# A fused gated block on one core: half of the attention's row transposes by DMA in int16 planes, the sums of |w3| in the last network

## The chip, the cores and the metric

The kernel runs on one core of a Trainium2 chip. The metric is the device time in microseconds of one execution; lower is better. Three executions of the kernel before gave 730.83, 730.84 and 731.93 us, median 730.84.

## The reference

`x` is 8 batches of 256 rows of 512, and the context has the same shape. Four steps each add to `x`, each weighted by the tanh of a gate:

```
x = x + tanh(g_xattn[0]) * long_convolution(ctx, ctx, layernorm(x))      # 32 heads of 8
x = x + tanh(g_ffn[0])   * ternary_network(layernorm(x), w1, w2, w3)     # 512 -> 1408 -> 512
x = x + tanh(g_xattn[1]) * attention(layernorm(x), ctx, mask)
x = x + tanh(g_ffn[1])   * sign_network(layernorm(x), w1, w2, w3)        # 512 -> 2048 -> 512

attention(h, m, mask): softmax(where(mask, h @ m.T / sqrt(512), -1e30)) @ m, zero where no key is valid
sign_network(h, w1, w2, w3):
    h = silu(lin(h, w1)) * lin(h, w2);  return lin(h, w3)
    lin(x, w) = quant(x) @ (sign(w) * mean(|w|)).T          # quant: 8 bits, one scale per 64 values
```

In the last network the mean of |w| is one number for a whole weight matrix. It scales the product from outside: the kernel multiplies by the signs and applies `mean(|w3|)` only where the result is added to `x`.

## The kernel before, in words

There are NT = 16 tiles of 128 rows, kept on the chip in `xs`. Five engines work from instruction streams whose order is that of the program text (`tc.manual_schedule()`): TensorE (PE), VectorE (DVE), ScalarE (ACT), GpSimd (POOL), and the queue of SyncE (SP), which issues nearly all DMAs. A wait in a stream holds all that follows in that stream. Tiles come from pools with a few buffers for each tag; a new tile with a tag waits until the readers of the tile that had its buffer are done.

**Convolution** (the first 182 us). A loop over 32 heads; jobs for the later stages are hung on heads with `job(h, slot, f)`: the statistics of the first rows for the first network (`first_stats`, `first_sqrt`, `first_inverse`, `first_by_act`), its weights, and the sums of |w1| and |w2| of the last network. Before it, `warm(n)` issues matmuls that nothing reads.

**First network** (to about 300 us). A loop over row tiles, each in three `up_block`s and a `down0`. `front_norm(t + 2)` normalises a tile that is used two tiles later, `ln_finish` turns the moments of four row tiles into `rstd` and `nmr` (a Newton iteration on POOL). From its fourth tile on, `w1_signs` also loads the last network's weights through `w1st` (three buffers of 256 KB) and takes their signs on ACT.

**Attention** (about 300 to 372 us). Row tile t goes through these steps, spread over iterations of the loop:
- `normalised3(t)` (ACT) makes the normalised rows; `x_transposed` turns them with four PE transposes into PSUM, and DVE copies them out, scaled by 1/sqrt(512), into `xT`.
- `scores` (PE, L938), `masked` (DVE, L946: adds the mask and takes the maximum), `exponentials` (ACT, L953).
- In the next iteration `e_transposed` turns the exponentials (PE, L959, and a copy by ACT, L961), and `readout` (PE, L967) multiplies them by the values. `residual` (DVE, L222) adds the result one iteration later.
- `load_keys`, `load_values` and `load_mask` fetch each batch of two row tiles. `signs`, `SIGNS[t]` at a time, are the remaining `w1_signs`. For the third matrix (i == 2) each also sums |w| (ACT, L842) into `w1sum3`. After all of them `total_w1(2)`, `spread` (a PE matmul that adds over partitions) and `mean_w1(2)` make the mean, and `gw1` is its product with the gate.

On PE an iteration has the order scores, transposes of e, transposes of x, readout. The first two of four blocks of tile 0 of the last network (`up_products` 0 and 1) are already done at the end of this loop.

**Last network** (372 to 728 us). A loop over the 16 row tiles. `up_products(xT, f)` for f = 0 to 3 makes the two products of 512 columns each (`pa`, `pb`) with the left side split in two parts, `hi` and `lo`; there are four PSUM banks for them (`ps_mm`), each freed by Silu (ACT, L1168) or by `up_gate` (DVE, L1172). After f = 1 and f = 3 `half_quantised` quantises half of the hidden row: DVE's scales and int16 values; on SP the scales' row to DRAM (`d`, L1293), the transpose of the values by DMA (`qT`, L1314) and two loads that spread the scales (`sT`, L1301). In tile t + 1 `hidden_high` makes `v = qT * sT` in the pool `p4` (tag `v`, two buffers), ACT's cast makes `hi`, DVE makes `lo`; `down` then multiplies the hidden rows of tile t - 1 by w3. So PE in tile t does up 0 to 3 of tile t and then `down` of tile t - 1. `finish` applies `gw1`, for the first time in tile 2.

```
            if t == 0:
                nxtT = split(pk, turned, "x1")
            g = up_products(xT, 3)
...
            halves.append(half_quantised(hh, 1))
            if 0 < t < NT - 1:
                po = new_out()
                down(po, hT, first if t == NT - 2 else range(NB))
```

The functions that the diff touches:

Of the kernel before, what the change touches and what calls it, by code (L numbers as in the profile page):

```python
# [9 lines left out]
F32 = mybir.dt.float32  # L10
# [3 lines left out]
I16 = mybir.dt.int16  # L14
# [7 lines left out]
P = 128  # L22
# [16 lines left out]
GRP = 4  # L39
# [3 lines left out]
def flamingo_gated_kernel(  # L43
# [115 lines left out]

    def ln_finish(got, g, tag):  # L160

        mv = got[g]
        v = small.tile([P, GRP], F32, tag="nwv", name="nwv")
        nc.vector.tensor_scalar(v, mv[:, :, 1], LN_EPS, None, ALU.add)
        i = small.tile([P, GRP], I32, tag="nwi", name="nwi")
        nc.vector.tensor_scalar(i, v.bitcast(I32), 1, None, ALU.arith_shift_right)
        y = small.tile([P, GRP], F32, tag="rstd" + tag, name="rstd")
        nc.vector.tensor_scalar(  # L170
            y.bitcast(I32), i, -1.0, float(0x5F3759DF), ALU.mult, ALU.add
        )
        w = small.tile([P, GRP], F32, tag="nwt", name="nwt")
        for _ in range(3):
            nc.gpsimd.tensor_tensor(w, y, y, ALU.mult)  # L175
            nc.gpsimd.tensor_tensor(w, w, v, ALU.mult)
            nc.gpsimd.tensor_scalar(w, w, -0.5, 1.5, ALU.mult, ALU.add)
            nc.gpsimd.tensor_tensor(y, y, w, ALU.mult)
        nmr = small.tile([P, GRP], F32, tag="nmr" + tag, name="nmr")
        nc.gpsimd.tensor_tensor(nmr, mv[:, :, 0], y, ALU.mult)  # L180
        nc.gpsimd.tensor_scalar(nmr, nmr, -1.0, None, ALU.mult)
        got[g] = (mv, y, nmr)

    def ln_some(got, order, k, tag):
        ln_moments_of(got, order, k, tag)
        if k % GRP == GRP - 1:
            ln_finish(got, k // GRP, tag)

# [429 lines left out]
    for k, h in enumerate(steps1):  # L618
        job(max(h - 2, steps1[k - 2] if k > 1 else 0), "late", load_w1a, k)
        job(h, "act2", abs_w1, k)  # L620
        if k % N1 == N1 - 1:
# [17 lines left out]

    for k, h in enumerate((24, 25, 28, 29)):  # L640
        job(h, "late", first_by_act, GRP + k)

# [28 lines left out]
    )  # L671
    warm(10)

# [135 lines left out]
    assert not jobs  # L809
    load_table(AF.Silu)  # L810

# [5 lines left out]

    ps_mm.tile([P, 512], F32, tag="mm", name="passed")

# [10 lines left out]
    def w1_signs(k):  # L830


        n = FF1 * L // P // 512
        i, c = k // n, k % n
        st = p_st.tile([P, 512], F32, tag="w1st", name="w1st")
        nc.sync.dma_start(out=st, in_=w1_part(i, c, 512))
# [29 lines left out]
    def down0(hqT):  # L866
# [17 lines left out]
        0: (st0, 1, "0"), 4: (st0, 2, "0"), 8: (st0, 3, "0"),  # L884
        13: (st3, 0, "3"), NT: (st3, 1, "3"),
    }
# [37 lines left out]
    def x_transposed(xn, by_act=False):  # L924
        tr = ps_tr.tile([P, NL, P], F32, tag="tr", name="tr3")
        for c in range(NL):
            nc.tensor.transpose(tr[:, c, :], xn[:, c * P : (c + 1) * P], ident)  # L927
# [55 lines left out]
    for t in range(NT + 1):  # L983
        new = t + 2 < NT
        if t < NT:
            hh = p2.tile([P, FF0], F32, tag="hh", name="hh")
        if new:
            front_norm(t + 2)
# [42 lines left out]
        if t > 2:  # L1031
            hqT, f3 = hq_.pop(t - 2)
            d_[t - 2] = (down0(hqT), f3)
        if t in FINISH:
            ln_finish(*FINISH[t])
# [17 lines left out]
        sums = []  # L1053
        if t == 0:
            clip_by_act(2, 3)
        if t == 3:
# [95 lines left out]
    def up_products(xT, f):  # L1152

        f0 = f * 512
        pa = ps_mm.tile([P, 512], F32, tag="mm", name="pa4")
        pb = ps_mm.tile([P, 512], F32, tag="mm", name="pb4")
        for i, pp in ((0, pa), (1, pb)):
            for c in range(NL):
                for k in range(2):
                    nc.tensor.matmul(  # L1160
# [16 lines left out]

    SIGNS = [2, 2, 2, 2, 1, 2, 1, 1, 2, 1, 2, 1, 1, 1, 1]
    e_, r_ = {}, {}
    for t in range(NT + 2):  # L1180
        if t >= 2:
            residual(t - 2, *r_.pop(t - 2))
        if t < NT and t not in ps_:
            ps_[t] = scores(xT_.pop(t), keys[t // 2])
        if 1 <= t <= NT:
            e, den = e_.pop(t - 1)
# [9 lines left out]
        if 1 <= t <= NT:  # L1196
# [12 lines left out]
        for make in signs:  # L1209
            make()  # L1210
        signs = []
        if t == NT:
            spread(("1", 2))
            up_gate(hh[:, 512:1024], *up_products(xT, 1))
# [12 lines left out]
        if t + 2 * GRP < NT:  # L1227
            ln_some(st3, natural, t + 2 * GRP, "3")
        elif t < 3 * GRP:
            ln_some(st4, natural, t - 2 * GRP, "4")  # L1230
# [7 lines left out]
        else:  # L1238
# [3 lines left out]
            if b + 1 < B:  # L1242
                negs[b + 1] = key_mask(bytes_.pop(b + 1))
        if t == NT - 1:
            total_w1(2)
        if t == NT:
            mean_w1(2)
            nc.vector.tensor_scalar(gw1, wmean1[:, 2:3], gate_f[1], None, ALU.mult)
        if t < len(SIGNS):
            signs = [w1_signs(made + k) for k in range(SIGNS[t])]  # L1250
            made += SIGNS[t]
# [19 lines left out]
    with ExitStack() as ph:  # L1271
# [89 lines left out]


        first, second = range(NB // 2), range(NB // 2, NB)
        prev, sums = None, []
        for t in range(NT):
# [6 lines left out]
            if t > 0:  # L1372
# [97 lines left out]
```

## Time and profile before

| | |
|---|---|
| median of three executions | 730.84 us |
| the profiled execution, its own time | 729.76 us |
| its span, first to last instruction | 728.0 us |
| PE busy | 716.1 us |
| DVE / ACT / POOL busy | 602.4 / 373.8 / 258.4 us |
| one attention iteration (readout to readout) | 4.39 us |
| tile of the last network on PE | 21.76 us |
| DMA, mean of the span | 136 GB/s |

A profiled execution has one clock from the start of the span; all moments in this text are on it. The busy shares say how full an engine is; the chain of waits goes back from the last instruction to whatever released each step; the timeline lists one engine's instructions with start, duration, line, output and inputs, and, in brackets, how long the engine idled before and for whom. The stretches give the busy time of each engine in a window, then the granted PE clock, the share of the DMA engines and the GB/s.

### The profile page before, as it was taken

The numbers are of one execution on the slowest core, as the hardware profiler recorded it, in microseconds if no ns is written. First come the engines' busy times: TensorE is split into PE (matmuls) and PEld (weight loads), VectorE is DVE, ScalarE is ACT, GpSimd is POOL, SyncE is SP. The second block draws the span as 40 slices with busy tenths as digits, with TensorE's granted clock in tenths as the row PEclk, the third lists the DMA queues.
The fourth block names the chain that finished last, engine by engine and source line by source line (L and its number), as shares of the span: only waits on it lengthen the run. The fifth ranks groups of instructions, "written<-read, shape, count | busy, mean of one in ns | idle before, by whom it ended". The sixth has DMA issues, their size and how long they took to land.

```text
span 728.0 us, 10153 instructions
## 1 busy us (share of the span) xinstructions
PE 716.1 (98%) x3212; PEld 533.8 (73%) x3212; DVE 602.4 (83%) x1224; ACT 373.8 (51%) x672; POOL 258.4 (36%) x363
## 2 busy tenths in 40 slices
PE   8999999999999999999999999999999999999997
PEld 7777777776454444566678788888888888888885
DVE  5799888998889887787867988988888988777965
ACT  5677887877778787777742322322212332212322
POOL 4888997989884525443300020000200002000000
PEclk9999999999999999999999999999999999999999
DMA  5774676831136576687605544555544544555443
GB/s 196 253 235 153 194 260 208 280 84 29 36 85 145 141 150 185 149 283 218 203 1 97 115 107 105 110 99 109 119 111 84 110 107 101 113 115 96 97 90 86
DMA packets 149970, 99.36 MB, mean 136 GB/s; under 512 B 83806, under 2 KB 127838, under 8 KB 149918
## 3 DMA queue, kind: packets, MB, share of 16 engines
q1 hardware_dynamic: 149608, 98.38, 53.5%
q0 software_dynamic: 256, 0.26, 0.4%
q8 instruction: 25, 0.41, 0.2%
q14 instruction: 27, 0.22, 0.1%
q10 hardware_dynamic: 54, 0.08, 0.1%
HBM read 75.58 MB, written 5.03 MB: 111 GB/s over the span
## 4 chain that ended last, share of the span: by engine, by line
PE 88%; DVE 4%; DMA 2%; ACT 2%; issue 1%; POOL 1%; SPq 0%; DVEq 0%; ACTq 0%
PE y L343 20%; PE po L1345 16%; PE pb L1160 15%; PE pa L1160 15%; PE po L869 5%; PE po L967 4%; PE pa L852 4%; PE pb L852 4%; PE ps L938 3%; PE tr_back L418 1%; DMA hqT<-qh 1%; DMA w1st<-in_L_w3t 1%; DVE am L512 1%; PE tr L927 1%; PE tr L410 1%
## 5 line engine op out<-in xcount | busy, mean ns | idle before, releaser
L343 PE MATMUL y<-kv,toep 128*128 128x288 f32 x640 | 160.7, 407 | 1.6 <-DVE rstd L128 0.8
L343 PEld LDWEIGHTS y<-kv,toep 128*128 128x128 f32 x640 | 119.3, 190 | 34.3 <-ACT y L353 2.1
L1168 ACT ACTIVATE sl<-pa,wmean 128x512 f32<-128x512 f32 x64 | 44.0, 688 | 187.5 <-PE pa L1160 187.5
L1160 PE MATMUL pa<-w,hi 128*128 128x512 f32 x256 | 100.6, 393 | 0.0
L1160 PE MATMUL pb<-w,hi 128*128 128x512 f32 x256 | 99.7, 390 | 0.4 <-DVE hh L1172 0.4
L1345 PE MATMUL po<-w,lo 128*128 128x512 f32 x256 | 99.9, 390 | 0.0
L1345 PE MATMUL po<-w,hi 128*128 128x512 f32 x256 | 99.6, 389 | 0.0
L1160 PE MATMUL pa<-w,lo 128*128 128x512 f32 x256 | 99.6, 389 | 0.0
L1160 PE MATMUL pb<-w,lo 128*128 128x512 f32 x256 | 99.6, 389 | 0.0
L175 POOL TENSOR_TENSOR nwt<-rstd 128x4 f32<-128x4 f32 x33 | 6.6, 199 | 241.5 <-DVE rstd L170 239.7
L320 POOL TENSOR_TENSOR kv<-cx 128x1024 f32<-128x1024 f32 x32 | 60.6, 1895 | 22.9 <-ACT cx L307 22.7
L852 PEld LDWEIGHTS <-xqT 128*128 128x128 bf16 x384 | 37.5, 98 | 40.0 <-issue 3.0
L388 POOL TENSOR_TENSOR prod<-prod 128x1024 f32<-128x1024 f32 x28 | 66.3, 2367 | 0.4 <-DVE prod L378 0.4
L1135 ACT CAST hi<-v 128x512 fp32r<-128x512 f32 x64 | 39.1, 621 | 48.3 <-DVE v L1335 48.3
L1172 DVE SCALAR_TENSOR_TENSOR hh<-pb,wmean,sl 128x512 f32<-128x512 f32 x64 | 47.7, 745 | 14.2 <-PE pb L1160 14.2
L1345 PEld LDWEIGHTS po<-w,lo 128*128 128x128 f32 x256 | 48.1, 188 | 10.9 <-DVE lo L1140 1.0
L1160 PEld LDWEIGHTS pb<-w,hi 128*128 128x128 f32 x256 | 48.0, 188 | 10.8 <-DVE hh L1172 0.8
L1160 PEld LDWEIGHTS pa<-w,hi 128*128 128x128 f32 x256 | 48.1, 188 | 10.4 <-issue 0.5
L1160 PEld LDWEIGHTS pa<-w,lo 128*128 128x128 f32 x256 | 48.1, 188 | 10.3 <-DVE lo L1140 0.2
L1160 PEld LDWEIGHTS pb<-w,lo 128*128 128x128 f32 x256 | 48.1, 188 | 10.0
L1345 PEld LDWEIGHTS po<-w,hi 128*128 128x128 f32 x256 | 48.0, 188 | 9.9
L365 DVE TENSOR_TENSOR prod<-y,qx 128x512 f32<-128x512 f32 x64 | 43.7, 683 | 9.3 <-ACT y L353 4.0
(160 smaller groups left out, 1350.8 us busy)
## 6 DMA issues: line engine op xcount, KB each, us to landing
sT<-d SPq DMA_DIRECT2D x64, 256.0 KB
toep<-ssm_skip SPq DMA_DIRECT2D x31, 256.0 KB
ch<-in_ctx_heads SPq DMA_DIRECT2D x32, 128.0 KB
w1a<-in_L_w1t SPq DMA_DIRECT2D x8, 512.0 KB
w1a<-in_L_w2t SPq DMA_DIRECT2D x8, 512.0 KB
w1st<-in_L_w1t SPq DMA_DIRECT2D x16, 256.0 KB
w1st<-in_L_w2t SPq DMA_DIRECT2D x16, 256.0 KB
cT<-in_ctx_t SPq DMA_DIRECT2D x8, 512.0 KB
```

The source lines that it names most:

```text
L320: nc.gpsimd.tensor_tensor(kv[:, :, 0 : ND * HD].rearrange("p a (i d) -> p a i d", d=ND), cx[:, :, 0:HD].unsqueeze(3).to_broadcast([P, NL * ...
L343: nc.tensor.matmul(y[:, k, :, W0 : W0 + NPAIR], toeps[h][:, d * P : (d + 1) * P], kvs[h][:, mi * B : (mi + 1) * B, :].rearrange("p b n -> ...
L365: nc.vector.tensor_tensor(prod[:, 0, r, :, :], yv[:, :, W0 : W0 + ND * HD].rearrange("p a (i d) -> p a i d", d=ND), view(q, [HX, n], [1, H ...
L388: nc.gpsimd.tensor_tensor(flat[0], flat[0], flat[1], ALU.add)
L852: nc.tensor.matmul(pp[:, :fw], xqT[:, c, :], w0q[i][:, c, f0 : f0 + fw], start=(c == 0), stop=(c == NL - 1),)
L869: nc.tensor.matmul(po, hqT[:, c, :], w0q[2][:, c, :], start=(c == 0), stop=(c == NF0 - 1))
L967: nc.tensor.matmul(po, eT[:, c, :], cN[:, c, :], start=(c == 0), stop=(c == S // P - 1))
L1135: nc.scalar.copy(hi, v)
L1160: nc.tensor.matmul(pp, xT[k][:, c, :], w1q[i][:, c, f0 : f0 + 512], start=(c == 0 and k == 0), stop=(c == NL - 1 and k == 1),)
L1168: nc.scalar.activation(sl, pa, AF.Silu, scale=wmean1[:, 0:1])
L1172: nc.vector.scalar_tensor_tensor(hh, pb, wmean1[:, 1:2], sl, op0=ALU.mult, op1=ALU.mult)
L1345: nc.tensor.matmul(po, hT[b][k][:, c, :], w1q[2][:, b * NL + c, :], start=(b == 0 and c == 0 and k == 0), stop=(b == NB - 1 and c == NL - ...
```

## The change

- In the attention, row tiles 4 to 15 are no longer turned by PE. POOL splits the normalised float32 rows into two planes of 2-byte integers, the low and the high halves of each value (`x_planes`); one DMA transpose on SP turns both (`x_turned`); DVE copies one plane and ACT the other back into float32 words (`x_merged`). The factor 1/sqrt(512), which the copy out of PSUM applied, goes into `rstd` and `nmr` in `ln_finish` for these rows (two more POOL instructions per group of four).
- `e_transposed` comes ahead of `scores` in iterations 1 to 15.
- The Abs sums of w3 leave `w1_signs`. In the last network `sums_of_w3` loads w3 a second time, 16 parts of 256 KB into the tag `v`, and sums each on ACT: parts 0 to 3 after the first half of tile 0, 4 to 7 after its second half, 8 to 15 after the second half of tile 1, followed by `total_w1(2)`, `spread`, `mean_w1(2)` and `gw1`.
- `SIGNS` is redistributed (the same sum), and signs wait one more iteration at the start.
- `up_products` goes over all four `hi` parts and then over the four `lo` parts.
- Smaller: the heads of `first_stats` and the like in the convolution; `warm(10)` becomes `warm(4)`; the Silu table is loaded by an activation that writes a PSUM tile; in tile 0 of the first network `front_norm(2)` and `ln_finish` come later.

```diff
-    def ln_finish(got, g, tag):
+    def ln_finish(got, g, tag, factor=None):
...
+        if factor is not None:
+            for v in (y, nmr):
+                nc.gpsimd.tensor_scalar(v, v, factor, None, ALU.mult)
...
-    for g, h in enumerate((22, 25)):
-        for k in range(2):
-            job(h + k, "dve", first_stats, 2 * g + k)
-        job(h + 1, "late", first_sqrt, g)
-        job(h + 2, "dve", first_inverse, g)
+    for g, (h0, h1, h2) in enumerate(((19, 21, 23), (23, 24, 28))):
+        job(h0, "dve", first_stats, 2 * g)
+        job(h1, "dve", first_stats, 2 * g + 1)
+        job(h1, "late", first_sqrt, g)
+        job(h2, "dve", first_inverse, g)
...
-    for k, h in enumerate((24, 25, 28, 29)):
-        job(h, "late", first_by_act, GRP + k)
+    for k, at in enumerate(((24, "late"), (25, "late"), (29, "act"), (30, "act"))):
+        job(*at, first_by_act, GRP + k)
...
-    warm(10)
+    warm(4)
...
-    load_table(AF.Silu)
...
-    ps_mm.tile([P, 512], F32, tag="mm", name="passed")
+    passed = ps_mm.tile([P, 512], F32, tag="mm", name="passed")
+    nc.scalar.activation(passed[:, :1], ln_eps, AF.Silu)
...
             nc.scalar.activation(dst, st, AF.Sign)
-            if i == 2:
-                nc.scalar.activation(st, st, AF.Abs, accum_out=w1sum3[:, c : c + 1])
...
+    def x_planes(xn):
+        pl = pt3.tile([P, 2, L], I16, tag="pl", name="pl")
+        nc.gpsimd.tensor_copy(pl, xn.bitcast(I16).rearrange("p (n k) -> p k n", k=2))
+        return pl.rearrange("p k n -> p (k n)")
+
+    def x_turned(pl):
+        bT = pt3.tile([P, 2 * NL, P], I16, tag="bT", name="bT")
+        nc.sync.dma_start_transpose(out=bT, in_=pl)
+        return bT.rearrange("p (k c) m -> p k (c m)", k=2)
+
+    def x_merged(b):
+        xT = p3.tile([P, NL, P], F32, tag="xT", name="xT")
+        v = xT.rearrange("p c m -> p (c m)").bitcast(I16).rearrange("p (n k) -> p k n", k=2)
+        nc.vector.tensor_copy(v[:, 1], b[:, 1])
+        nc.scalar.copy(v[:, 0], b[:, 0])
+        return xT
...
-        if new:
+        if new and t > 0:
             front_norm(t + 2)
...
             up_block(*x0[t], hh, 0)
+        if t == 0:
+            front_norm(t + 2)
...
         for i, pp in ((0, pa), (1, pb)):
-            for c in range(NL):
-                for k in range(2):
+            for k in range(2):
+                for c in range(NL):
...
-    SIGNS = [2, 2, 2, 2, 1, 2, 1, 1, 2, 1, 2, 1, 1, 1, 1]
+    SIGNS = [1, 2, 2, 2, 2, 2, 1, 1, 2, 1, 2, 1, 1, 1, 1]
...
     for t in range(NT + 2):
+        if t + 2 in pl_:
+            bT_[t + 2] = x_turned(pl_.pop(t + 2))
+        if t == NT - 2:
+            xT_[t + 1] = x_merged(bT_.pop(t + 1))
+        if 1 <= t <= NT:
+            e, den = e_.pop(t - 1)
+        if 1 <= t < NT:
+            eT = e_transposed(e)
         if t >= 2:
             residual(t - 2, *r_.pop(t - 2))
         if t < NT and t not in ps_:
             ps_[t] = scores(xT_.pop(t), keys[t // 2])
...
-        if t + 2 < NT:
+        if t + 2 < GRP:
             xT_[t + 2] = x_transposed(xn_.pop(t + 2))
         if t < NT:
             e_[t] = exponentials(*s_nmx)
-        if t + 3 < NT:
+        if t + 1 in bT_ and t < NT - 2:
+            xT_[t + 1] = x_merged(bT_.pop(t + 1))
+        if t + 3 < GRP:
             xn_[t + 3] = normalised3(t + 3)
-        for make in signs:
-            make()
-        signs = []
+        elif t + 3 < NT:
+            pl_[t + 3] = x_planes(normalised3(t + 3))
+        if t > 0:
+            for make in signs:
+                make()
+            signs = []
...
-        if t == NT - 1:
-            total_w1(2)
-        if t == NT:
-            mean_w1(2)
-            nc.vector.tensor_scalar(gw1, wmean1[:, 2:3], gate_f[1], None, ALU.mult)
...
+        def sums_of_w3(cs):
+            for c in cs:
+                st = p2.tile([P, NL, P], F32, tag="v", name="w3st").rearrange("p c m -> p (c m)")
+                nc.sync.dma_start(out=st, in_=w1_part(2, c, 512))
+                nc.scalar.activation(st, st, AF.Abs, accum_out=w1sum3[:, c : c + 1])
...
             halves = [half_quantised(hh, 0)]
+            if t == 0:
+                sums_of_w3(range(0, 4))
...
             halves.append(half_quantised(hh, 1))
+            if t == 0:
+                sums_of_w3(range(4, 8))
+            if t == 1:
+                sums_of_w3(range(8, 16))
+                total_w1(2)
+                spread(("1", 2))
+                mean_w1(2)
+                nc.vector.tensor_scalar(gw1, wmean1[:, 2:3], gate_f[1], None, ALU.mult)
             if 0 < t < NT - 1:
                 po = new_out()
                 down(po, hT, first if t == NT - 2 else range(NB))
```

More of the change, by code (lines that the diff above doesn't have):

```diff
@@ L181, in ln_finish, with ln_some @@
         nc.gpsimd.tensor_scalar(nmr, nmr, -1.0, None, ALU.mult)
+        if factor is not None:
+            for v in (y, nmr):
+                nc.gpsimd.tensor_scalar(v, v, factor, None, ALU.mult)
         got[g] = (mv, y, nmr)
-    def ln_some(got, order, k, tag):
+    def ln_some(got, order, k, tag, factor=None):
         ln_moments_of(got, order, k, tag)
         if k % GRP == GRP - 1:
-            ln_finish(got, k // GRP, tag)
+            ln_finish(got, k // GRP, tag, factor)
     def ln_apply(o, t, mv, rstd, j):
@@ L884, in flamingo_gated_kernel @@
         0: (st0, 1, "0"), 4: (st0, 2, "0"), 8: (st0, 3, "0"),
-        13: (st3, 0, "3"), NT: (st3, 1, "3"),
+        13: (st3, 0, "3"), NT: (st3, 1, "3", scale),
     }
@@ L1033, in flamingo_gated_kernel @@
             d_[t - 2] = (down0(hqT), f3)
-        if t in FINISH:
+        if t in FINISH and t > 0:
             ln_finish(*FINISH[t])
@@ L1054, in flamingo_gated_kernel @@
         if t == 0:
+            ln_finish(*FINISH[t])
             clip_by_act(2, 3)
@@ L1174, in up_gate @@
         )
-    SIGNS = [2, 2, 2, 2, 1, 2, 1, 1, 2, 1, 2, 1, 1, 1, 1]
-    e_, r_ = {}, {}
+    SIGNS = [1, 2, 2, 2, 2, 2, 1, 1, 2, 1, 2, 1, 1, 1, 1]
+    e_, r_, pl_, bT_ = {}, {}, {}, {}
+    pt3 = pool(s_att, "p3turn", 2, reuse_waits="tile")
     for t in range(NT + 2):
+        if t + 2 in pl_:
[6 more added lines that the diff above has]
+            eT = e_transposed(e)
         if t >= 2:
@@ L1185, in flamingo_gated_kernel @@
         if 1 <= t <= NT:
-            e, den = e_.pop(t - 1)
             fac = small.tile([P, 1], F32, tag="fac", name="fac")
@@ L1195, in flamingo_gated_kernel @@
             up_gate(hh[:, 0:512], *up_products(xT, 0))
-        if 1 <= t <= NT:
+        if t == NT:
             eT = e_transposed(e)
@@ L1206, in flamingo_gated_kernel @@
             e_[t] = exponentials(*s_nmx)
-        if t + 3 < NT:
+        if t + 1 in bT_ and t < NT - 2:
+            xT_[t + 1] = x_merged(bT_.pop(t + 1))
+        if t + 3 < GRP:
             xn_[t + 3] = normalised3(t + 3)
-        for make in signs:
-            make()
-        signs = []
+        elif t + 3 < NT:
[4 more added lines that the diff above has]
+            signs = []
         if t == NT:
-            spread(("1", 2))
             up_gate(hh[:, 512:1024], *up_products(xT, 1))
@@ L1227, in flamingo_gated_kernel @@
         if t + 2 * GRP < NT:
-            ln_some(st3, natural, t + 2 * GRP, "3")
+            ln_some(st3, natural, t + 2 * GRP, "3", scale)
         elif t < 3 * GRP:
@@ L1243, in flamingo_gated_kernel @@
                 negs[b + 1] = key_mask(bytes_.pop(b + 1))
-        if t == NT - 1:
-            total_w1(2)
-        if t == NT:
-            mean_w1(2)
-            nc.vector.tensor_scalar(gw1, wmean1[:, 2:3], gate_f[1], None, ALU.mult)
         if t < len(SIGNS):
-            signs = [w1_signs(made + k) for k in range(SIGNS[t])]
+            signs += [w1_signs(made + k) for k in range(SIGNS[t])]
             made += SIGNS[t]
```

## The prediction

> **What bounds the kernel now.** I read the page's busy shares first, then the chain of waits, then the timelines of TensorE (PE), ScalarE (ACT), VectorE (DVE) and the SP queue around the attention and the first tiles of the last network.
>
> ```profile
> PE 716.1 (98%) x3212; PEld 533.8 (73%) x3212; DVE 602.4 (83%) x1224; ACT 373.8 (51%) x672; POOL 258.4 (36%) x363
> PE 88%; DVE 4%; DMA 2%; ACT 2%; issue 1%; POOL 1%; SPq 0%; DVEq 0%; ACTq 0%
> ```
>
> PE is busy for 98% of the span and carries 88% of the chain that ends last. So a saving counts only if it takes PE work away or closes one of PE's few gaps, and whatever makes PE wait is paid in full. One attention iteration on PE:
>
> ```profile
> 335.41 1.98 PE L967 MATMUL po<-cN,eT 128*128 128x512 f32 x4
> 337.23 1.89 PE L938 MATMUL ps<-cT,xT 128*128 128x256 f32 x8
> 338.95 0.38 PE L959 MATMUL tre<-ident,s 128*128 128x128 f32 x2
> 339.17 0.60 PE L927 MATMUL tr<-ident,xn 128*128 128x128 f32 x4
> 339.80 1.98 PE L967 MATMUL po<-cN,eT 128*128 128x512 f32 x4
> ```
>
> From readout to readout it is 4.39 us; the four transposes of x take 0.44 of it in the chain. The last network before the change, first SP and then ACT:
>
> ```profile
> 383.90 0.69 SPq L1293 DMA_DIRECT2D d<-sq  x1
> 385.19 1.25 SPq L1314 DMA_TRANSPOSE qT<-qh  x1
> 386.62 1.34 SPq L1301 DMA_DIRECT2D sT<-d  x2
> ...
> 377.80 0.69 ACT L1168 ACTIVATE sl<-pa,wmean 128x512 f32<-128x512 f32 x1 [1.70 <-PE pa L1160]
> 383.19 0.69 ACT L1168 ACTIVATE sl<-pa,wmean 128x512 f32<-128x512 f32 x1 [4.70 <-PE pa L1160]
> 385.45 0.59 ACT L1135 CAST hi<-tr 128x512 fp32r<-128x512 f32 x1 [1.57 <-PE tr L1149]
> 387.30 0.69 ACT L1168 ACTIVATE sl<-pa,wmean 128x512 f32<-128x512 f32 x1 [1.26 <-PE pa L1160]
> ```
>
> SP issues in the order of the program: the row `d`, the transpose `qT`, the two `sT`. ACT idles a lot there, but it too runs in program order, and each Silu (`sl`) and cast (`hi`) is what PE needs next.
>
> **What the Trainium skill says.** "DMA: Bandwidth & Descriptors", in Anatomy of one DMA: "any semaphore wait happens on the issuing sequencer before dispatch". The trace agrees: in the waits of the SP queue, line L836 (the weight loads) stands 11.1 us behind ACT's sums at L842. The same section fits a DMA of the gpsimd path as 2.0 us plus bytes/436 GB/s, an estimate of 2.6 us for 256 KB. This trace, for SP's queue:
>
> ```profile
> 212.87 2.15 SPq L836 DMA_DIRECT2D w1st<-in_L_w1t  x2
> 213.50:214.00 0.50, 0.50 (x4) 0.20 (x3) 0.43 (x3) 0.50 (x2) 0.50 (x1) 1.00 0.04 5
> 214.00:214.50 0.50, 0.50 (x5) 0.21 (x3) 0.35 (x2) 0.50 (x2) 0.50 (x1) 1.00 0.38 135
> 217.00:217.50 0.50, 0.50 (x5) 0.24 (x3) 0.47 (x3) 0.45 (x1) 0.41 (x2) 1.00 0.26 98
> ```
>
> The issue starts at 212.87, the bytes (last column, GB/s) at 214.0, and the two loads of 256 KB, one after the other, are through at 217.4: 1.1 us to the first byte, about 1.7 us each. I take **2.8 us** from issue to landing; bounds 2.3 (bytes at the 390 GB/s of other stretches) and 5.1 (the `w1st` DMA that the chain shows at 318.54, in traffic). "TensorE: Matmul & The Clock Gate", Part 1: after an idle window of about 3.4 us PE runs at half rate until about 3.4 us of work have passed. The trace agrees in kind: the warming matmuls of 128x128 run 0.216 us apart (20 in 4.31 us), the same shape at L927 later 0.109.
>
> **The sums of |w3|, moved.** Before, each of 16 loads of `w3` (`w1st`) feeds both a Sign and an Abs on ACT (0.72 us with its accumulator read) during the attention. After, the Abs are gone from there, and 16 new loads of 256 KB feed 16 Abs in tiles t=0 and 1 of the last network. They share tag `v`, two buffers, so load k waits on SP for sum k-2; they stand on SP behind `d`, `qT`, `sT` of the half just quantised, and on ACT ahead of the next Silu. I walk it on the clock of the trace before.
>
> *Tile 0, sums 0 to 3.* SP is free at 388.0 (386.62 + 1.34). The engines move `sT` until 390.6 (the stretches there), so loads 0 and 1 land at 391.3 and 392.0. Sums 0 and 1 end at 392.05 and 392.8; loads 2 and 3 go out then and land 2.8 later; sum 3 ends at 396.35. Only now ACT reaches the Silu that ran at 383.19, then the cast that ran at 385.45: done at 397.65. PE had four PSUM banks ahead and finishes `up_products` 3 at 389.1; the first product of tile 1 needs that cast. PE starts at 397.7: **8.6 us late**.
>
> *Sums 4 to 7.* DVE, behind the Silu, multiplies gate 3 from 399.3; as before, 4.07 us later the half is quantised (403.4), then `qT` 1.25 and `sT` 1.3 with the 0.35 between them: SP is free at 406.3. The engines move `sT` to 408.7, load 4 lands at 409.4, sum 5 ends at 410.85, loads 6 and 7 land at 412.95 and 413.7, sum 7 ends at 414.4. ACT's first Silu of tile 1 follows, to 415.1. PE has done two `up_products` (3.63 each) by 405.0 and waits for a PSUM bank until 415.1: **10.1 us**.
>
> *Sums 8 to 15, then `total_w1`, `spread`.* PE finishes products 2 and 3 of tile 1 at 422.4. DVE was held too (the `v` of `hidden_high` wait for the same buffers): from 414.5 it does two `v`, gate, two `lo`, two `v`, gate, the first half's quantising (3.2), two `lo`, gate, `xn`, statistics, gate, `lo` to 427.5, by the durations of its timeline before; the second half is quantised at 430.6, SP is through `sT` at 433.5. Load 8 lands at 436.6, and four pairs follow, each at 2.8 + 0.72 (+0.05): sum 15 ends at 448.7. The reduce (0.17), the matmul `tot` (0.28) and hand-offs: 449.3. `spread` stands on PE **ahead of** `down`, which ran at 404.30 before: everything after is **45.0 us** later. From there PE is dense in both kernels, so nothing is won back. Restarting cold: first restart hidden in the second wait, second behind DVE, third counts 3.4/2 = 1.7 us (bounds 0 and 4). The later `gw1` and 4 MB more traffic cost nothing else: the first use of `gw1` is tile 2, behind the wait already counted.
>
> **The attention.** For 12 rows PE loses four transposes: 12 x 0.44 = 5.3 us at most. The copy `eT` after the transpose of the exponentials, which ends just when the transposes of x do, would stand open; moving `e_transposed` ahead of `scores` (1.73) covers it. New iteration on PE: 1.98 + 1.73 + 0.23 = 3.95. Who else must fit in 3.95?
> - DVE: row 4.39 minus its gaps is near 3.7; `xT` (0.69) is replaced by an int16 copy of 512 elements, not in the trace. I take 0.6, bounds 0.3 and 0.7, nearest row the 0.69 of L1107. Fits.
> - ACT: `eT` 0.44, exponentials 0.6, normalising 0.7, the other plane 0.65 (as L1135), Signs 0.64 each, no Abs: 3.7 with two Signs. Its order makes `eT` late with two, period about 4.0 to 4.1.
> - POOL: `x_planes`, 1024 elements, not in the trace: 1.0 (rate of L1018, 1408 in 1.36) to 1.9 (L320, 1024 in 1.90); I take 1.4. With masks and `ln_finish` under 3.5. The two more multiplies of `ln_finish` are 0.4 per four rows, hidden by the 3 to 6 us POOL idles before it.
> - DMA: a transpose of this size is `qT`, issued in 1.25 and through in 2.7 us, about 1.5 us of all engines. Keys and values 1.3, signs' loads 0.67 each: 3.5 with one Sign, 4.1 with two.
> - SP's order: `x_turned` precedes the next keys and w-loads; a loop row, plane, transpose, merge takes 7 to 9 us for two iterations.
>
> So I take 4.05 instead of 4.39: 12 x 0.34 = **4 us gained**, bounds 5.3 gained and 3 lost.
>
> **The small edits together.** Six fewer warming matmuls (PE stood in them until 10.0 while the first normalised row was there about 8.0), `front_norm` behind the first Silu, `ln_finish` behind the first block, the statistics of conv spread: PE's gaps there are 0.8 (167.9), 0.95 (182.7), 0.2, 0.6 (193.1) and up to 2 at the start. **2 us gained**, bounds 0 and 4.5. The new order hi, then lo in `up_products`: nothing, `lo` is already there in all but one tile. `SIGNS` keeps its sum.
>
> **Sum.** 45.0 + 1.7 - 4 - 2 = +40.7 on the profiled execution's own 729.76 (span 728.0 and 1.76 around it) = 770.5. That execution lies 1.1 below the median of 730.84; I forecast **771**.
>
> **Rivals.**
> - *Only the last wait is open* (ACT is through its sums of tile 0 before PE needs it): 771 - 18.7 = 752. For it: ACT idles 4.7 us before 383.19. Against: the loads can't be issued before 388.0. 0.05.
> - *The sums are hidden, the kernel is faster*: only the gains count, 730.84 - 6 = 725. One mechanism decides, the in-order SP queue with its two buffers: if the loads ran ahead so that sum 15 ended before PE leaves `up_products` of tile 1 at 404.3, nothing waits. For it: DMA is about half busy and ACT 30% there. Against: SP's order in the trace, 45 us too late by my walk. 0.06.
> - *The attention does not gain* (transposes land late and hold `scores`, or DMA is the bound): 771 + 7 = 778. For it: DMA shares near 1.0 at 320 to 331. 0.07.
> - My forecast, own range 758 to 786: 0.82.
>
> A measurement of this kernel can tell about 0.2% (1.5 us) from no change. Faster 0.06, same 0.01, slower 0.93. The range: low end, 8 round trips at 2.3 (-4), all gains at their bounds (-3.8), no cold restart (-1.7) and part of the first wait hidden (-9); high end, round trips a microsecond longer (+8), no gain in the attention (+7), a colder PE (+2): 752 to 788.
>
> **What would show it.** PE idle three times in the last network's first two tiles, about 9, 10 and 27 us, released by ACT `hi`, ACT `sl` and the `tot` matmul's DVE total; `v<-in_L_w3t` loads on SP in pairs 3.6 us apart; ACT waiting for that DMA; attention rows 4.0 us apart. It is wrong if PE stays dense between 372 and 412, or if the gap ahead of `down` is under 15 us.

## The result, and the profile after

Four executions of the changed kernel took 788.18 to 789.57 us, median **789.01 us**, against 730.84 for the kernel before: a ratio of 1.0796, 95% interval 1.0781 to 1.0811. The change costs 58 us. The profiled execution has a span of 787.0 us instead of 728.0, and a mean PE clock of 0.971.

The page of the kernel after, the busy shares first, then two rows of the 40 slices (19.7 us each; busy share of PE and PE's granted clock, both in tenths), then the chain by engine:

```profile
PE 718.2 (91%) x3139; PEld 532.3 (68%) x3152; DVE 598.3 (76%) x1224; ACT 380.6 (48%) x684; POOL 272.3 (35%) x381
...
PE   7999999999999998888954159999999999999997
...
PEclk9999999999999999999977769999999999999999
...
PE 71%; DMA 7%; DVE 6%; POOL 6%; issue 4%; ACT 4%; SPq 1%; ACTq 0%; DVEq 0%; POOLq 0%
```

PE did not get more work: its busy time is 2.1 us above the 716.1 of before, in a span 59 us longer. It lost its cover: 71% of the chain instead of 88%. In the row of PE the slices with 5, 4, 1 and 5 are one place, 393 to 472 us, and there the clock is at 7, 7, 7 and 6 tenths. The three waits, from PE's timeline of that place (start, duration, line, what; in brackets how long PE idled before it and for whom):

```profile
407.26 2.07 PE L1183 MATMUL pa<-w,hi 128*128 128x512 f32 x4 [9.72 <-ACT hi L1157]
426.20 2.08 PE L1183 MATMUL pa<-w,hi 128*128 128x512 f32 x4 [9.94 <-ACT sl L1191]
460.46 0.56 PE L218 MATMUL tot<-wtot,ones 128*128 128x1 f32 x2 [24.53 <-DVE wtot L213]
```

Together 44.2 us of idle PE. What PE waited for, from the chain of waits of the same stretch (start, duration, what):

```profile
396.28 4.85 DMA w3st<-in_L_w3t
401.21 0.73 ACT w3st L1399 x2
401.96 2.70 DMA w3st<-in_L_w3t
404.74 0.66 ACT w3st L1399 x2
...
443.14 4.45 DMA w3st<-in_L_w3t
447.68 0.73 ACT w3st L1399 x2
448.42 2.75 DMA w3st<-in_L_w3t
...
456.36 2.96 DMA w3st<-in_L_w3t
459.40 0.73 ACT w3st L1399 x2
460.46 0.56 PE tot L218 x2
461.02 9.33 PE po L1376 x32
```

Load, sum, load, sum: with two buffers each pair of loads starts when a sum of the pair ahead of it has ended. `down` (the last line) took 9.33 us here and 7.25 in the kernel before, although it is the same 32 matmuls:

```profile
404.30 7.25 PE po L1345 x32
```

PE starts it cold here: on its timeline the first matmuls lie 0.43 us apart, and from 465.2 on 0.23. The waits of the stretch (total, times, longest):

```profile
ACT w3st L1399 <- DMA w3st<-in_L_w3t: 49.8, 11, 14.3
...
DVE wtot L213 <- ACT w3st L1399: 19.7, 1, 19.7
```

Where the 59.0 us of span came from, by the moments at which PE starts the first product of each stage, each rounded to a tenth:

| stage | before | after | difference |
|---|---|---|---|
| convolution, to its last product | 181.3 | 185.2 | +3.9 |
| from there to the first product of the first network | 1.4 | 0.2 | -1.2 |
| first network, to the first `scores` | 115.7 | 117.9 | +2.2 |
| attention, to the first `up_products` | 72.8 | 76.6 | +3.8 |
| to the first `down` | 32.9 | 81.0 | +48.1 |
| the rest | 323.9 | 326.1 | +2.2 |

### The profile page after: what moved, and what is told of

Read it like the earlier page. It is cut to its first block, busy times and chain, and to the rows that moved or that the text cites. A ratio compares the mean times of both kernels' runs of the same rounds, so it can differ in the third digit from the quotient of the medians.

```text
span 787.0 us, 10144 instructions
## 1 busy us (share of the span) xinstructions
PE 718.2 (91%) x3139; PEld 532.3 (68%) x3152; DVE 598.3 (76%) x1224; ACT 380.6 (48%) x684; POOL 272.3 (35%) x381
## 4 chain that ended last, share of the span: by engine, by line
PE 71%; DMA 7%; DVE 6%; POOL 6%; issue 4%; ACT 4%; SPq 1%; ACTq 0%; DVEq 0%; POOLq 0%
PE po L1376 15%; PE y L346 14%; PE pa L1183 14%; PE pb L1183 14%; PE po L869 4%; DMA w3st<-in_L_w3t 4%; PE pa L852 4%; PE pb L852 3%; POOL prod L391 1%; DMA hqT<-qh 1%; PE po L986 1%; PE ps L957 1%; POOL kv L323 1%; DMA bT<-pl 1%; DMA xs<-in_x 1%
## 5 line engine op out<-in xcount | busy, mean ns | idle before, releaser
L1183 PE MATMUL pa<-w,hi 128*128 128x512 f32 x256 | 71.5, 402 | 19.7 <-ACT sl L1191 9.9
L1183 PE MATMUL pa<-w,lo 128*128 128x512 f32 x256 | 70.0, 396 | 0.0
L1183 PE MATMUL pb<-w,hi 128*128 128x512 f32 x256 | 69.0, 392 | 0.0
L1183 PE MATMUL pb<-w,lo 128*128 128x512 f32 x256 | 68.5, 390 | 0.0
L1183 PEld LDWEIGHTS pb<-w,lo 128*128 128x128 f32 x256 | 48.1, 188 | 10.0
```

Source lines behind the costliest of these rows:

```text
L1183: nc.tensor.matmul(pp, xT[k][:, c, :], w1q[i][:, c, f0 : f0 + 512], start=(c == 0 and k == 0), stop=(c == NL - 1 and k == 1),)
```

## The experiments

My theory (A) was the prediction's: the sums of w3 as they stand in the last network cost nearly all, by SP's order and two buffers; the open question was the attention, which did not gain as forecast. The rival (B) for each part is in the expectations. All ratios are against the kernel before, run on the same chip.

**1. The sums alone, both ways.** `e1_sums_only` is the kernel before with only the sums moved; `e2_sums_back` is the kernel after with only the sums put back into the attention.

```diff
             nc.scalar.activation(dst, st, AF.Sign)
-            if i == 2:
-                nc.scalar.activation(st, st, AF.Abs, accum_out=w1sum3[:, c : c + 1])
...
+            if t == 0:
+                sums_of_w3(range(0, 4))
...
+            if t == 1:
+                sums_of_w3(range(8, 16))
+                total_w1(2)
+                spread(("1", 2))
+                mean_w1(2)
```

> The kernel before with only the sums of w3 moved to the last network, as in the change. Theory A (three waits in tiles 0 and 1, as walked in the prediction): PE idles about 9.7, 9.9 and 24.5 us there, down starts about 48 us later than before, restart cold adds 2; the whole takes about 780 us (+50). Rival B (the moved sums cost much of it through ACT or DMA traffic all along, or the attention without its sums wins some of it back): under 770 us, or waits of another length.

> The changed kernel with the sums of w3 put back into the attention, as before. Theory A: the three waits vanish, what is left is the loss up to the end of the attention, 4.9 us before it and 4.0 in it, so about 740 us, or a few us more if ACT's sums (0.72 each) make the copies of the exponentials later still. Rival B (the attention and the small edits are a gain that the sums only hide): 725 to 729 us.

Measured: e1 782.06 us, ratio 1.0702 (1.0682 to 1.0721); e2 740.17 us, ratio 1.0142 (1.0111 to 1.0172). So the move of the sums is worth about +51 us in the kernel before and, taken out of the kernel after, 49; all other edits together, with the sums where they were, are worth **+9**, not a gain. In e1, with none of the other edits present, PE's timeline has the same three waits with the same releasers: 9.34 us for ACT `hi`, 8.82 for ACT `sl`, and this one:

```profile
456.18 0.56 PE L215 MATMUL tot<-wtot,ones 128*128 128x1 f32 x2 [24.21 <-DVE wtot L210]
```

**2. The two buffers.** `e8_sums_hidden` is e1 with other loads: parts 0 to 7 go out ahead of the last network's loop into tiles of the hidden blocks that are idle there, parts 8 to 15 into the same tiles later; the sums are spread over tiles 0 and 1. `e9_after_hidden` does the same to the kernel after.

```diff
-                st = p2.tile([P, NL, P], F32, tag="v", name="w3st").rearrange("p c m -> p (c m)")
-                nc.sync.dma_start(out=st, in_=w1_part(2, c, 512))
+                tag = ("hih", "loh")[c % 2] + str(c // 2 % 4)
+                w3st[c] = p1.tile([P, 512], F32, tag=tag, name="w3st")
+                nc.sync.dma_start(out=w3st[c], in_=w1_part(2, c, 512))
...
+        load_w3(range(8))
```

> The kernel before with the sums of w3 in the last network, but with their loads ahead: parts 0 to 7 are loaded before tile 0 into tiles that are idle until tile 1 (hi and lo of the hidden blocks), parts 8 to 15 as soon as these are summed, and the sums stand behind Silus after which ACT is idle. Theory A (the moved sums cost only through in-order waits for late loads): the three waits vanish, 729 to 733 us, the same as before within 0.3%. Rival B (16 sums and 4 MB more traffic there cost by themselves): 740 us or more.

> The changed kernel with the same loads ahead. Theory A: what remains of the change is the attention (3.9 us longer than before), the first network (about 2 longer) and the end of the convolution (about 1 shorter): 735 to 738 us. Rival B (without the waits the change is a gain): under 729 us.

Measured: e8 741.15 us, ratio 1.0145 (1.0130 to 1.0160); e9 746.01 us, ratio 1.0212 (1.0196 to 1.0227). Of the 51 us, 41 are gone with the same 4 MB and the same Abs: most of the price was loads and sums that waited for each other in order. The run changes both the buffers of the loads and the places of the sums on ACT, so it does not part these two. Some 10 us stayed: I had expected at most 733 for e8 and 738 for e9, and e8 lies in the range of its rival (740 or more). The chain of waits of e8 says where:

```profile
383.48 0.08 SPq L1362
...
383.61 4.70 DMA w3st<-in_L_w3t
...
398.42 5.06 DMA d<-sq
...
404.29 4.78 DMA sT<-d
...
409.80 0.69 DVE v L1327
...
411.20 3.76 PE pb L1158 x8
```

The burst of eight loads could not leave "ahead of the loop": it went out only at 382.8 to 383.5, when the last residual of the attention released the memory that those tiles take over. From there it stood in front of everything else in the queue: the row of scales `d`, which is small, needed 5.06 us to land (in the kernel before, the loads that wait for it go out 2.7 and 3.1 us after its issue). The loads `sT` behind it took 4.78, little more than the 4.50 of the same step before. PE waits 6.2 us for that (6.07 in e9, at the same place), and its next eight matmuls, cold, take 3.76 us (1.84 before). The loads are hidden from ACT and come out again as late scales: the same queue, another victim.

**3. The planes.** `e7_planes_undone` is the kernel after with rows 4 to 15 turned by PE again, `scores` still behind `e_transposed`; the two additional multiplies of `ln_finish` go too (not shown).

```diff
-        if t + 2 < GRP:
+        if t + 2 < NT:
             xT_[t + 2] = x_transposed(xn_.pop(t + 2))
...
-        if t + 3 < GRP:
+        if t + 3 < NT:
             xn_[t + 3] = normalised3(t + 3)
-        elif t + 3 < NT:
-            pl_[t + 3] = x_planes(normalised3(t + 3))
```

> The changed kernel with the rows turned by PE again (x_transposed for all), everything else as changed: the transposes of e ahead of scores, no sums of w3 in the attention, the new SIGNS. Theory A (the planes are what costs): the attention takes 72 to 73 us as in the kernel before, the whole about 4 us less than the changed kernel, 785 us. Rival B (the new order, e_transposed ahead of scores, costs): it stays near 76.6 us, 789.

Measured: 779.38 us, ratio 1.0672 (1.0640 to 1.0704), and an attention of 69.7 us, against 76.6 with the planes and 72.8 before. **Taking the four transposes off PE in this way made the attention 6.9 us longer.** (Each of these figures is from one profile. The same attention differs by up to 0.8 us between profiles: 72.8 before and 73.2 in e3, 72.3 in e10 and 73.1 in e11.) In e7 a row on PE, from its timeline:

```profile
348.28 1.88 PE L986 MATMUL po<-cN,eT 128*128 128x512 f32 x4
...
351.95 0.60 PE L927 MATMUL tr<-ident,xn 128*128 128x128 f32 x4
352.38 1.88 PE L986 MATMUL po<-cN,eT 128*128 128x512 f32 x4
```

4.10 us, and no wait. The kernel after, same view, three of its waits:

```profile
342.20 1.98 PE L986 MATMUL po<-cN,eT 128*128 128x512 f32 x4 [1.52 <-ACT eT L980]
...
357.26 2.00 PE L957 MATMUL ps<-cT,xT 128*128 128x256 f32 x8 [0.84 <-ACT xT L951]
...
360.71 1.99 PE L986 MATMUL po<-cN,eT 128*128 128x512 f32 x4 [1.46 <-ACT eT L980]
```

**4. Why the planes are late.** Two candidates: the DMA queue (the Signs' loads `w1st` and the transposes share it) and the order of POOL. `e5_no_w3_loads` leaves out 15 of the 16 `w1st` loads of w3; `e6_short_newton` takes two of three Newton steps from `ln_finish` for the rows from 4 on; `e6b_short_no_loads` does both.

```diff
-        st = p_st.tile([P, 512], F32, tag="w1st", name="w1st")
-        nc.sync.dma_start(out=st, in_=w1_part(i, c, 512))
+        if i == 2 and c > 0:
+            st = kept[0]
...
-        for _ in range(3):
+        for _ in range(1 if tag == "3" and g > 0 else 3):
```

> The changed kernel, but in the attention the signs of w3 are taken 16 times from one loaded part; the other 15 loads of 256 KB are left out, ACT's 16 Signs stay (so the signs of w3 are those of one part). Theory A (the DMA engines are the bound of the new attention: with the transposes they are full, the w-loads land late, the Signs wait and hold the copy eT that readout needs): the waits of readout for eT L980 (5.4 us in the changed kernel) shrink to 1 us or less and the attention takes about 72 us from the first scores to the first product of the last network instead of 76.6. Rival B (ACT's own work and order, or POOL's): it stays within 1 us of 76.6.

> The changed kernel with one Newton step instead of three in ln_finish for the attention's rows from the fifth on (less exact rstd; 8 POOL instructions of 0.28 us fewer each time). Theory A (POOL's order: ln_finish stands ahead of the next plane copy, so the transpose is issued late and scores wait for xT, as at 344 to 357 us in the changed kernel): the waits of scores for xT and what they delay shrink, the attention takes 1 to 2 us less than 76.6. Rival B (only the DMA engines bound it): within 0.5 us of 76.6.

> The same, and the signs of w3 taken from one loaded part, so 15 loads of 256 KB are left out as well. If DMA and POOL's order are the two causes together: the attention falls to 68 to 71 us, waits of PE for eT and xT under 1 us in all. If it stays above 73, a third cause (ACT's order with the plane copy in it, or the latency of plane, transpose and merge) holds it.

Measured: e5 785.69 us, ratio 1.0754 (1.0736 to 1.0772), attention 74.6; e6 784.57 us, 1.0734 (1.0707 to 1.0762), attention 73.9; e6b 782.72 us, 1.0717 (1.0689 to 1.0744), attention 71.7. Each alone gives back a part (2.0 and 2.7 us of the 6.9), both together 4.9. Neither theory alone was right; the part of each is small against a spread of 0.8, the sum of both is not. POOL's part is seen in the kernel after, in the chain of waits of one row:

```profile
344.04 1.03 POOL pl L939
345.07 0.17 POOL nwt L175
...
349.57 0.22 POOL nmr L184
...
349.87 1.08 POOL neg L908
...
351.01 1.15 POOL pl L939
352.18 4.17 DMA bT<-pl
...
356.43 0.78 ACT xT L951
...
357.26 2.01 PE ps L957 x8
```

Between two plane copies POOL has a whole `ln_finish`, in instructions of 0.2 us, and a mask conversion: 5.9 us. The second row was normalised at 348.8 (ACT's timeline), so its copy, at 351.0, is 2.2 us late, on an engine that is busy for 38 of the 67 us around. Then comes a transpose that needs 4.17 us to land.

The queue's part is in the DMA view, packets in the attention's main stretch of 65 us before and 67 after:

```profile
DMA packets 7718, 13.72 MB, mean 211 GB/s; under 512 B 2113, under 2 KB 2113, under 8 KB 7713
```

```profile
DMA packets 20387, 16.86 MB, mean 252 GB/s; under 512 B 14782, under 2 KB 14782, under 8 KB 20382
```

The planes bring 3.1 MB, 23% more, but 12,669 small packets; in the stretch's windows the DMA share rises from 0.68 to 0.96. The engines are nearly full, and the Signs' loads are late. On ACT the copy `eT` stands behind them:

```profile
340.46 0.63 ACT L842 ACTIVATE w<-w1st 128x512 fp32r<-128x512 f32 x1 [1.94 <-DMA w1st<-in_L_w3t]
...
341.79 0.35 ACT L980 COPY eT<-tre 128x256 f32<-128x256 f32 x1
```

In all the Signs wait 7.5 us for their loads in the kernel after, 2.2 before and 0.2 in e5. In e5 the waits of readout for `eT` fall from 5.4 us to 0.3, as theory A said; but `scores` now waits 2.2 us until `eT` is done and still 1.8 for `xT`, and the attention is only 2 us shorter. The transposes did not land sooner without the loads: 4.2 and 4.3 us in e5's chain, at a DMA share of 0.83.

There is a third suspect that no run here parts from the other two: the order on SP. `x_turned` is issued first in an iteration, and SP stands there until POOL has the plane; keys, values and the Signs' loads are held behind it. Of the waits of SP from 310 to 376 us:

```profile
SPq L944 <- POOL pl L939: 12.7, 7, 4.1
```

With the waits there for POOL's `ln_finish` and mask it is 22.0 us; in the kernel before SP has no such wait. From 347.97 to 352.18, for example, SP stands so, and the load behind it, issued at 354.14, is the one for which a Sign waits 1.89 us at 359.77. e5 takes away both the traffic and the loads that stand behind SP.

The 2.0 us that e6b leaves are in the last two rows. From the second readout to the thirteenth e6b takes 45.7 us, e7 45.8; from there to the next readout 7.9 against 5.4. e6b's chain shows the same picture once more, since its three Newton steps for the *last* network's first group are still there:

```profile
356.82 0.17 POOL nwt L175
...
360.88 1.08 POOL neg L914
...
362.02 1.05 POOL pl L945
...
363.08 3.06 DMA bT<-pl
...
367.05 1.99 PE ps L963 x8
```

**5. ACT's share.** `e13_merge_dve` is e6b with both planes copied back by DVE, none by ACT.

```diff
         nc.vector.tensor_copy(v[:, 1], b[:, 1])
-        nc.scalar.copy(v[:, 0], b[:, 0])
+        nc.vector.tensor_copy(v[:, 0], b[:, 0])
```

> The run with one Newton step and without the loads of w3, and both plane copies on DVE instead of one on ACT. Theory A (ACT's order is the third cause: its plane copy of 0.65 us stands between the exponentials and the normalising of the row that POOL, DMA and the merge then have to bring in two iterations): the attention falls from 71.7 to 70 us or less. Rival B (the latency of plane, transpose and merge, or DVE, which becomes full): 71.5 us or more.

Measured: 785.98 us, ratio 1.0746 (1.0729 to 1.0763), attention 75.0: 3.3 us longer than in e6b. As a whole it came out on the rival's side. Yet the rows between are the fastest of all kernels:

```profile
347.70 1.88 PE L992 MATMUL po<-cN,eT 128*128 128x512 f32 x4
...
351.36 1.89 PE L992 MATMUL po<-cN,eT 128*128 128x512 f32 x4
```

3.66 us a row: this is what the planes can give, 0.44 less than e7's 4.10, the four transposes. Five rows run so. The others wait, up to 1.54 us behind DVE's part of `ln_finish`, and 2.55 us for the last row's `xT`, whose plane left POOL at 365.4, behind an `ln_finish` and a mask again. So with ACT's copy the planes do not beat PE's transposes (e6b's rows are 4.10 apart on average), and without it the order on DVE and POOL takes the gain back.

**6. The order alone, and a version that beats both.** `e10_e_ahead` is the kernel before with only `e_transposed` ahead of `scores`; `e11_e_ahead_conv` adds the edits at the end of the convolution; `e12_e_ahead_signs` is e10 with the Signs dealt so that no row after the second carries more than one until the last three.

```diff
+        if 1 <= t <= NT:
+            e, den = e_.pop(t - 1)
+        if 1 <= t < NT:
+            eT = e_transposed(e)
...
-    SIGNS = [2, 2, 2, 2, 1, 2, 1, 1, 2, 1, 2, 1, 1, 1, 1]
+    SIGNS = [3, 3, 1, 1, 1, 1, 1, 1, 1, 1, 1, 1, 2, 2, 2]
```

> The kernel before with e_transposed ahead of scores in iterations 1 to 15 and nothing else; the rows turned by PE, the sums of w3 in the attention. Theory A (the gain of the run with the planes undone, 4.10 us per iteration instead of 4.39, is that of the order: readout no longer waits for eT): 3 to 4 us less, 727 to 728 us. Rival B (that gain came from ACT being rid of the sums; with them eT is late): 730 to 731 us.

> The same with the change's edits of the convolution's end as well (statistics on other heads, the Silu table loaded by the activation that writes a PSUM tile), but the first network in its old order. Theory A: the first block of the first network starts 1.2 us sooner after the last product of the convolution, and the wait in front of its third block stays 0.6 us instead of 1.9: about 1 us less than the run with the order alone. Rival B: no difference that can be told.

> The kernel before with e_transposed ahead of scores, and the signs spread evenly: three in each of the first two iterations, then one, and two in the last three. Theory A (in the run with the order alone, readout still waited 0.3 to 0.7 us for eT wherever two signs and two sums of w3 stood ahead of it on ACT): these waits vanish, the attention takes 70 to 71 us instead of 72.3, the whole 1 to 2 us less than that run, 728 to 730 us. Rival B (three signs in the first iterations hold the eT there, or the last ones hold the first product of the last network): no gain, 731 us.

Measured: e10 730.73 us, ratio 0.9992 (0.9981 to 1.0004); e11 731.02 us, 1.0000 (0.9989 to 1.0011); e12 **728.69 us, 0.9972 (0.9961 to 0.9982)**. In e10 the gain is there in rows with one Sign, and taken back in those with two, where PE waits for `eT` behind two Signs and two Abs on ACT, 0.68 us and three times 0.32; two of the four lines of its timeline:

```profile
327.89 1.98 PE L967 MATMUL po<-cN,eT 128*128 128x512 f32 x4 [0.68 <-ACT eT L961]
...
336.68 1.98 PE L967 MATMUL po<-cN,eT 128*128 128x512 f32 x4 [0.32 <-ACT eT L961]
```

e12 has ten rows from 321.1 to 362.3, 4.13 apart (4.39 before), and pays 0.5 and 1.2 us in the two rows with three Signs. It is 0.28% faster than the kernel before and the only one here that beats both. The attention of e10 is 0.5 us shorter than before, which is within the spread of one profile. e11's edits bring the first product of the first network 1.1 us nearer to the convolution (0.3 instead of 1.4 us), and the time does not change: its first product of a later block waits 0.67 us for DVE where e10's waits 0.22.

**7. The start.** `e3_warm4_only` is the kernel before with `warm(4)`, `e4_warm10` the kernel after with `warm(10)`.

```diff
-    warm(10)
+    warm(4)
```

> The kernel before with six fewer warming matmuls and nothing else. Theory A (PE enters the first transposes and products cold): the first stretch of unbroken convolution products begins about 2 to 3 us later, 733 to 734 us. Rival B (the late start in the changed kernel was a slow first load of x in that one execution): 729 to 731 us, with the transposes 0.11 us apart.

> The changed kernel with ten warming matmuls instead of four. Theory A (cold start): 2 to 3 us less than the changed kernel, about 786 us. Rival B (slow load): within 0.5 us of the changed kernel, 789.

Measured: e3 731.45 us, ratio 1.0014 (1.0003 to 1.0025); e4 784.97 us, ratio 1.0743 (1.0722 to 1.0763). By the numbers the two disagree. e3 came out on the rival's side: fewer warming matmuls gain nothing; if anything they lose 0.14%. e4 came out on theory A's: it is 4 us below the kernel after, and the intervals of their ratios do not touch. The profiles speak for the slow load of x. The long unbroken stretch of products begins at 17.2 us in e4 and at 17.3 in e3, with four warming matmuls, but at 21.5 in the kernel after; there DVE waits 5.26 and later 1.14 us for the loads of x, against 4.7 before and 4.6 in e3 and e4. The last product of the convolution starts at 185.2 in the kernel after and at 181.2 in e4; in the seven other profiles with the changed convolution and four warming matmuls it starts between 181.8 and 184.5, in the five with the convolution of before between 181.3 and 184.3. So a good part of the +3.9 is a spread between executions, and how much belongs to the change is not settled. It also touches the comparisons with the kernel after: e5, e6, e6b, e7 and e13 are 1.1 to 2.7 us faster than it beyond what their attention explains.

## Why the prediction was right and where it failed

The direction and the mechanism of the large part were right; the time lies 18 us above the forecast, above its range (758 to 786) and above the sum of its worst cases (788). Of the 18 us, 7.8 are the attention, 6.9 the small edits with the start, 3.5 the waits and the restart. The sum's terms (the measured ones in the profiled execution):

| term | forecast | measured |
|---|---|---|
| `down` of tile 0 late, three waits | +45.0 | +48.1 |
| cold restart | +1.7 | +2.1 |
| attention | -4 | +3.8 |
| small edits and start | -2 | +4.9 (3.9 - 1.2 + 2.2) |

**The waits.** 8.6, 10.1 and about 27 us were forecast, released by ACT `hi`, ACT `sl` and DVE's total; 9.7, 9.9 and 24.5 came, released by just these. The pairs of loads are 3.7 us apart; 3.6 were forecast. The walk on the queues of SP and ACT therefore stands, and e1 shows it alone (+51). What it had too small: the first load of each batch, which I had land 3.1 to 3.3 us after SP was free, took 4.85, 4.86 and 4.45: the DMA engines, with `sT` just issued ahead, were busy throughout (share 0.84 to 1.11 from 396.5 to 400.5), but at 178 to 236 GB/s. That is 4.7 us over the three batches, of which 1.6 were won again on the way. What the Trainium skill's "DMA: Bandwidth & Descriptors", Anatomy of one DMA, says of the wait on the issuing sequencer holds here too: SP's `w3st` loads waited 19.7 us for ACT.

**The cold restart.** I took half of the 3.4 us window that the prediction cites, 1.7 us. Measured: 9.33 - 7.25 = 2.1; PE ran slow for 4.7 us, from 460.5 to 465.2. The earlier two restarts did cost PE clock, as the row of PEclk shows, and were indeed hidden in the next wait: the chain of waits has no piece of PE between 393.9 and 460.4.

**The attention** is the step that failed: the prediction put the chain that brings one row from its normalising to `scores` at nothing, because two iterations seemed to cover it. It cost more than the four transposes gave: turned by PE again, the attention is 6.9 us shorter (e7). Four parts of it:
- The iteration was mis-sized: I summed the readout as 1.98, the duration of its row, though instructions on PE overlap by some 0.2. Without transposes a row is 3.66 (e13), with them 4.10 (e7). The gain at stake was twice what I took.
- I asked whether each engine's *load* fits in an iteration, and took it that it does, though my own 4.1 for DMA with two Signs lay above the 4.05 of the row. I did not walk the *chain* of one row: normalise, POOL's plane copy, transpose, two copies, `scores`. I put it at 7 to 9 us for two iterations, which are 8.1, and left it at that. In the kernel after, the row shown under 4 took 9.25 us, from 348.01 to 357.26: its plane copy came 2.2 us late behind `ln_finish` and a mask on POOL. "POOL under 3.5" was true (37.8 us in 67, about 2.5 a row) and no answer: a mean doesn't say who stands in front. Nor did I ask what SP would hold back while it stands at `x_turned`.
- The plane copy took 1.03 us (1.4 taken), the copies 0.53 on DVE and 0.76 on ACT (0.6 and 0.65). The transposes took 3.1 and 4.2 us to landing in the chain, where I had 2.7 and no bound above it.
- The relief of ACT, 16 Abs gone, was real in the new order: the sums back in place (e2) make an attention of 80.5 us, with 59.0 us of work for ACT instead of 48.6. With PE's own transposes, relief and new order together give 3.1 us against before (e7). Neither does so alone: the order gives 0.5 (e10, attention 72.3), and the relief nothing (e1, attention 74.2, its rows 4.44 us apart).

The rival "the attention does not gain" had the right cause, late transposes, and the bound for it, 3 lost, fell 0.8 short.

**The small edits** failed too. In the first network PE's gap ahead of the third block's second product grew from 0.63 to 1.90 us:

```profile
197.12 0.81 PE L852 MATMUL pb<-w,xqT 128*128 128x384 bf16 x4 [1.90 <-DVE hh L861]
```

`ln_finish` does not stand behind the first block, as I had read, but behind the third block of the first tile. It puts about 1.9 us of DVE work (192.5 to 194.4) between the last gate `hh` of that tile and the first of the next, where before it lay ahead of both. I had taken the gap for something that the move would close. The rest of the first network's +2.2 is a wait for `hqT`, 1.23 instead of 0.31.

What stays open: the 3.9 us of the convolution, as told, and whether loads of w3 sent still earlier, in small lots between the rows of scales, would hide the sums whole; no run here shows it. Nor is it shown how the loss of the planes divides between the traffic and SP's order.

## What to carry to other kernels

Work that is "free" on an idle engine still needs a place in every queue that it passes: walk each new load from its issue to its reader, and count whose small transfers stand behind it; two buffers on an in-order queue turn sixteen loads into eight round trips. For a step that leaves the bounding engine, don't add up loads per engine: follow one row through the new chain, with what is in front of it on each engine. And order the side work evenly first: here the transposes of e ahead and the Signs dealt one to a row gained 0.28% (e12), while the planes lost 6.9 us.

## What I had not expected of the hardware

- A small transfer waited behind large ones: the row `d` landed 5.06 us after its issue behind eight loads of 256 KB (e8), and in at most 2.7 and 3.1 us without them (before).
- The DMA transposes of 12 planes of 256 KB came to some 12,700 packets under 512 bytes, six times those of all other transfers in the stretch, and raised the DMA share from 0.68 to 0.96 for 3.1 MB.
- In the kernel after, the first load of 256 KB of each batch, right behind `sT`, took 4.45 to 4.86 us of the chain, the later ones 2.70 to 2.96.
